# Joining two projection weights, turning softmax weights through DRAM, and a bias product by array quarters in a mixture-of-experts kernel

## The chip, the cores and the metric

The kernel runs on one core of one Trainium2 chip, in f32 throughout. The metric is the device time of one launch in microseconds; the median of three runs of the kernel before is 474.62 us (474.44 to 474.79).

## The reference

Eight batches of 512 tokens of width 256 attend to 64 context rows each; a router then mixes three experts, and a gate multiplies the result. Cut to what matters:

```python
nx = layer_norm(x, ln_gamma, ln_beta)                 # (8, 512, 256)
q, k, v = nx @ Wq, context @ Wk, context @ Wv         # context (8, 64, 256)
weights = softmax(q @ k.T * H ** -0.5)                # (8, 512, 64)
evidence = weights @ v
combined = concat([nx, evidence, anchor])             # anchor: one row for each batch
probs = softmax(combined @ router_W + router_b)       # 3 experts
h = silu(combined @ e_w1 + e_b1)                      # (8, 512, 3, 512)
routed = sum((h @ e_w2 + e_b2) * probs)
g = sigmoid(silu(combined @ gate_w1 + gate_b1) @ gate_w2 + gate_b2)
out = x + g * (routed @ out_w + out_b)
```

## The kernel before

**Work and order.** Batches go in four pairs, j = 0 to 3. Before the loop comes a start: the context and the attention weights are loaded and projected, and the first pair is normalized, scored and softmaxed. Then for every pair come the gate's first layer, three expert layers (e = 0, 1, 2, each with points A to D) and the outputs (points named "begin", "gate", P1, P5, P6, P2, P7, P3, P4 in that order). The order on every engine is written out by hand: instructions stand in each engine's queue in the order in which the program issues them, and an engine works its queue in that order. Small steps for the next pair are hung on the points by `put(within, ...)` and `put(between, ...)` (lines 1119 to 1184). Products over a pair of batches are made by a scheme of seven products with sums and differences (`nx_product`, `product`, line 657), with tokens as 512 columns.

**Attention.** q is never made. `context_transposes` turns the context, `project_keys` (line 303) makes the keys kT from Wk, `wq_transposes` (line 285) turns Wq, and `project(wqT, kT, keep_m, "m")` (line 1088) makes m = Wq k, so that `scores` (line 522) multiply the normalized x by m. The result m lies in mr beside the router's rows for x. The values vT come from `project(wv_sb, ...)` (line 1079); `value_weights` (line 623) multiplies them by the experts' first weights, so that evidence enters the experts as softmax weights times a 64-row product (`evidence`, line 664). For that the softmax weights w must stand with context rows on partitions: `transpose_w` (line 557) does it with four TensorE transposes to PSUM and a ScalarE copy (line 566), for pair 0 in the gate layer and for the later pairs at point P7 of the pair before.

**The start's order.** SyncE's queue loads the context in two halves, then x of batch 0, Wq, x of batch 1, then the first-layer weights (lines 1059 to 1071). ScalarE's queue loads Wk and Wv. VectorE makes statistics of x (`statistics`, line 450), ScalarE the deviation (line 461, which needs a table load for Sqrt), VectorE normalizes (line 469); TensorE transposes x (line 491). `small_transposes` (line 257) turns the bias rows into `cols` and the condition into condT; `router_anchor` (line 324) needs condT.

**Blocks.** VectorE's transpose turns 32x32 blocks. Where a whole turn is wanted, `load_blocks` (line 382) loads from DRAM with the blocks already regrouped, one DMA for 32 partitions, and VectorE turns each block. x of the later batches goes that way: `store_x` (line 494), `regroup_x` (line 498), `transpose_blocks` (line 503). Outputs are turned the same way in `finish` (line 957), and SyncE stores them.

**Biases.** `second_bias` (line 431) multiplies the experts' second biases by out_w once, at point B of expert 0 of pair 0. `anchor_rows` (line 347) multiplies by the condition in array quarters: a 32-column stationary operand, with the result on partitions 32 i to 32 i + 31 of PSUM, and a VectorE transpose that turns it back.

**Pools.** The large tiles of the hidden layer double as scratch in the start (scr_w, scr_k, scr_ctx). The tiles w, wT and vw of the work pool have one buffer each, yb has two. `misc` and `either` (lines 103 and 244) hand out PSUM banks in rotation.

Of the kernel before, what the change touches and what calls it, by code (L numbers as in the profile page):

```python
# [8 lines left out]
F32 = mybir.dt.float32  # L9
# [7 lines left out]
def kernel(  # L17
# [85 lines left out]
    def misc(name):  # L103
        spare.append(spare.pop(0))
        return bank(spare[-1], name)
# [26 lines left out]
    def rows_of(w):  # L132
        return w.rearrange("(k p) n -> p k n", p=P)
# [8 lines left out]
    def by_k(flat, n):  # L142
        return flat.rearrange("p (k n) -> p k n", n=n)
# [3 lines left out]
    scr = scratch(1, 1, "scr_w")  # L147
    wk_sb, wq_sb, wqT, wv_sb = (by_k(scr[:, i * KH * H : (i + 1) * KH * H], H) for i in range(4))
    scr = scratch(0, 2, "scr_k")
    kT = by_k(scr[:, :HK], B * CT)  # L150
    rrow = scr[:E, HK : HK + B]
    scr = scratch(0, 0, "scr_wa0")
    wa = {0: by_k(scr[:, :HK], RH), E: by_k(scr[:, HK : HK + KH * H], H)}
# [90 lines left out]
    def either(name):  # L244
        turn[0] += 1
        return bank((1, 2, 0, 3)[turn[0] % 4], name)
# [10 lines left out]
    def small_transposes():  # L257
        pt = either("pt_rows")
        nc.tensor.transpose(pt[:, :NR], rows, ident[:NR, :NR])
        nc.vector.tensor_copy(cols, pt[:, :NR])  # L260
        pt = either("pt_cond")
        for k in range(KH):
            nc.tensor.transpose(
                pt[:, k * B : (k + 1) * B], cond_sb[:, k * P : (k + 1) * P], ident[:B, :B]
            )
        nc.vector.tensor_copy(
            condT[:, :, :B], pt[:, : KH * B].rearrange("p (k b) -> p k b", b=B)
        )
# [13 lines left out]
            half = slice(d * NX // 2 * P, (d + 1) * NX // 2 * P)  # L282
            (nc.scalar.copy if d else nc.vector.tensor_copy)(ctxT[:, :, half], pt)

    def wq_transposes():
        pt = either("pt_wq")
        for k in range(KH):
            for i in range(KH):
                nc.tensor.transpose(
                    pt[:, k * H + i * P : k * H + (i + 1) * P], wq_sb[:, i, k * P : (k + 1) * P], ident  # L290
                )
        nc.scalar.copy(wqT.rearrange("p k n -> p (k n)"), pt)

    def project(w_sb, src, evacuate, name):
        for m in range(KH):
            ps = either(f"ps_{name}_{m}")
            for k in range(KH):
                nc.tensor.matmul(  # L298
                    ps, w_sb[:, k, m * P : (m + 1) * P], src[:, k, :], start=(k == 0), stop=(k == KH - 1)
                )  # L300
            evacuate(m, ps)

    def project_keys():

        ps = [either(f"ps_k_{m}") for m in range(KH)]
        for d in range(2):
            half = slice(d * NX // 2 * P, (d + 1) * NX // 2 * P)
            for m in range(KH):
                for k in range(KH):
                    nc.tensor.matmul(  # L310
                        ps[m][:, half], wk_sb[:, k, m * P : (m + 1) * P], ctxT[:, k, half],
                        start=(k == 0), stop=(k == KH - 1),
                    )
        for m in range(KH):
            nc.scalar.copy(kT[:, m, :], ps[m])

    def keep_m(m, ps):
        nc.vector.tensor_copy(mr[:, m, :, :CT], ps.rearrange("p (b c) -> p b c", c=CT))
# [54 lines left out]
    w2o = const.tile([P, NE, H], F32, tag="w2o", name="w2o")  # L373
    w2s = const.tile([P, 3, NE // 2, P], F32, tag="w2s", name="w2s")
    b2o = const.tile([P, KH, E], F32, tag="b2o", name="b2o")
    ow_sb = const.tile([P, KH, H], F32, tag="ow_sb", name="ow_sb")
    gw2_sb = const.tile([P, KH, H], F32, tag="gw2_sb", name="gw2_sb")
    gw2s = const.tile([P, 3, P], F32, tag="gw2s", name="gw2s")
# [3 lines left out]
    def load_blocks(dst, src):  # L382

        for k in range(KH):
            for i in range(P // TB):
                lo = k * P + i * TB
                nc.sync.dma_start(
                    dst[i * TB : (i + 1) * TB, k, :].rearrange("r (j c) -> r j c", c=TB),  # L390
                    src[:, lo : lo + TB].rearrange("(j r) c -> r j c", r=TB),
                )
# [37 lines left out]

    def second_bias():

        ps = misc("ps_b2o")
        for i in range(KH):
            for k in range(KH):
                nc.tensor.matmul(
                    ps[:, i * E : (i + 1) * E], ow_sb[:, k, i * P : (i + 1) * P], b2_c[:, :, k],
                    start=(k == 0), stop=(k == KH - 1),
                )
        nc.vector.tensor_copy(b2o, ps[:, : KH * E].rearrange("p (i e) -> p i e", e=E))  # L440
        for i in range(KH):
            nc.vector.tensor_scalar(
                b2o[:, i, 1:], b2o[:, i, 1:], b2o[:, i, 0:1], None, ALU.subtract
            )
        nc.vector.tensor_tensor(b2o[:, :, 0], b2o[:, :, 0], ob_c, ALU.add)
# [105 lines left out]
    def softmax(b):  # L551
        w, sm = S["w", b // 2][:, :, b % 2, :], S.pop(("sm", b))
        rs = work.tile([P, NT], F32, tag="rs", name=f"rs_{b}")
        nc.vector.reciprocal(rs, sm)
        nc.vector.tensor_tensor(w, w, rs.unsqueeze(2).to_broadcast([P, NT, CT]), ALU.mult)

    def transpose_w(j):

# [498 lines left out]
    with tc.manual_schedule(engines=None):  # L1057
        ctx_rows = context.flatten_outer_dims().rearrange("(t p) d -> p t d", p=P)
        for d in range(2):
            half = slice(d * NX // 2, (d + 1) * NX // 2)  # L1060
            nc.sync.dma_start(ctx_sb[:, half, :], ctx_rows[:, half, :])
        nc.scalar.dma_start(wk_sb, rows_of(Wk))
        nc.scalar.dma_start(wv_sb, rows_of(Wv))
        load_x(0)
        nc.sync.dma_start(wq_sb, rows_of(Wq))
        load_x(1)
        for g in (E, 0):
            load_first(g)
# [3 lines left out]

        wake(7)
        context_transposes()
        project_keys()
        statistics(0, 0, NT)
        deviation(0, 0)
        normalize(0)
        project(wv_sb, ctxT, lambda m, ps: nc.scalar.copy(vT[:, m, :], ps), "v")
        small_transposes()  # L1080
        wq_transposes()
        transpose_x(0)
        router_anchor()
        statistics(1, 0, NT)
        deviation(0, 1)
        normalize(1)
        load_table(AF.Exp)
        project(wqT, kT, keep_m, "m")
        combine_weights(E)
        value_weights(0, E)  # L1090
        spread_router_rows(0)
# [22 lines left out]
        for j in range(NP):  # L1114
# [37 lines left out]
            if j + 1 < NP:  # L1152
                b0, b1 = 2 * j + 2, 2 * j + 3
                put(within, "gate", load_x, b0)
                put(within, "gate", load_x, b1)
                put(within, (0, "A" if j else "D"), statistics, b0, 0, NT)
                put(within, (0, "C") if j else (1, "A"), statistics, b1, 0, NT)
                for i in range(2):
                    put(within, (1, "C"), deviation, j + 1, i)
                where = (1, "D") if j else (2, "B")  # L1160
                put(within, where, normalize, b0)
                put(within, where, store_x, b0)
                put(within, where, regroup_x, b0)
                put(within, (2, "C"), normalize, b1)
                put(within, (2, "C"), store_x, b1)
                put(between, "begin", transpose_blocks, b0)
                put(between, "gate", regroup_x, b1)
                put(between, "P1", scores, b0)
                put(between, "begin", value_weights, j + 1, E)
                put(between, "begin", spread_router_rows, j + 1)  # L1170
                put(between, "P5", softmax, b0)
                put(between, "P5", transpose_blocks, b1)
                put(between, "P6", router_logits, b0)
                put(between, "P2", scores, b1)
                put(between, "P2", softmax, b1)
# [47 lines left out]
```

## Time and profile before

| What | Value |
|---|---|
| Median of three runs | 474.62 us |
| The profiled execution | 474.75 us |
| Its span, first to last instruction | 473.0 us |
| Granted TensorE clock over the span | 1.0 |
| DMA engines' mean busy share from 10.4 to 15.7 us | 1.08 |
| The same from 135 to 140 us | 0.30 |
| TensorE busy from 21 to 28 us | 6.71 of 7.00 us |
| VectorE busy from 125 to 155 us | 27.51 of 30.00 us |

The profile is of one execution. Times are microseconds from the span's start. PE is TensorE's matmul, PEld its weight load, DVE is VectorE, ACT is ScalarE, POOL is GpSimd, SPq is SyncE's queue of DMA issues. Busy time counts time in which at least one instruction of the engine runs. A chain piece gives its start and length; the chain is followed back from the last instruction, at each step to what released it, or to the instruction before it on its engine. A timeline line gives start, length, engine, line and operation, output and inputs with their shapes, and in brackets the idle time just before with its releaser. A DMA line gives the issue alone; its landing is in another view. One f32 matmul instruction appears as two records on TensorE, a transpose as one. "x16" means 16 records.

### The profile page before, as it was taken

The page shows a single profiled execution, that of the slowest core. Times are in us where ns is not written, and L with a number is a line of the kernel's source. Part 1 is how long each engine was busy: PE and PEld are TensorE (multiplying, and loading weights), DVE is VectorE, ACT ScalarE, POOL GpSimd, SP SyncE. Part 2 cuts the span into 40 slices and gives each one's busy share as a digit, 9 for nine tenths or more (in the row PEclk, how much of TensorE's full clock was granted, in tenths as well). Part 3 has the DMA queues.
Part 4 walks back from the last instruction along what each step waited for, and adds up shares of the span by engine and source line. Part 5 has one row for each costly group of instructions (what it writes and reads, how often), then busy time and mean ns, then how long its engine had stood idle before and what let it go on. Part 6 is the DMA issues. An engine that isn't in the chain of part 4 may idle for free.

```text
span 473.0 us, 4654 instructions
## 1 busy us (share of the span) xinstructions
PE 467.0 (99%) x1447; PEld 222.8 (47%) x1447; DVE 353.3 (75%) x649; ACT 218.3 (46%) x391; POOL 85.7 (18%) x109
## 2 busy tenths in 40 slices
PE   8999999999999999999999999999999999999997
PEld 6654546445454444445454444445454344444454
DVE  2855846989989555889989565898989624797982
ACT  3555656557221546648320456758221365458000
POOL 5328133200062300000062300000042400000020
PEclk9999999999999999999999999999999999999999
DMA  9988330057211740342111750252111560000013
GB/s 289 366 130 162 54 136 0 0 110 105 27 22 25 164 147 0 82 97 45 17 24 22 158 154 1 66 113 46 18 22 22 84 184 0 1 0 1 0 22 67
DMA packets 118504, 35.27 MB, mean 75 GB/s; under 512 B 105164, under 2 KB 115472, under 8 KB 117968
## 3 DMA queue, kind: packets, MB, share of 16 engines
q1 hardware_dynamic: 114736, 27.02, 27.7%
q0 software_dynamic: 1856, 7.18, 5.1%
q10 hardware_dynamic: 1888, 0.79, 0.6%
q8 instruction: 11, 0.18, 0.2%
q14 instruction: 13, 0.11, 0.1%
HBM read 27.57 MB, written 7.40 MB: 74 GB/s over the span
## 4 chain that ended last, share of the span: by engine, by line
PE 92%; DVE 5%; DMA 1%; ACT 1%; issue 0%; SPq 0%; ACTq 0%; DVEq 0%
PE ps_u L657 42%; PE ps_z L657 18%; PE ps_y L657 15%; PE ps_vw L632 5%; PE ps_gu L657 3%; PE ps_w2o L415 2%; PE ps_s L530 2%; PE ps_gz L657 1%; DVE h L931 1%; DMA scr_ctx<-in_ctx_dram 1%; DVE h L740 1%; PE ps_k L310 1%; PE ps_gy L657 1%; PE ps_v L298 1%; ACT w L545 1%; DVE r L940 0%
## 5 line engine op out<-in xcount | busy, mean ns | idle before, releaser
L740 DVE TENSOR_TENSOR h<-h,pb 128x512 f32<-128x512 f32 x96 | 61.9, 694 | 10.5 <-ACT h L690 10.5
L657 PE MATMUL ps_u<-h,w2o 128*128 128x512 f32 x144 | 63.9, 593 | 0.0
L657 PE MATMUL ps_u<-nxT,w 128*128 128x512 f32 x112 | 55.6, 607 | 0.0
L690 ACT ACTIVATE h<-h,abias 128x512 f32<-128x512 f32 x72 | 49.3, 718 | 8.7 <-DVE h L696 8.2
L657 PE MATMUL ps_z<-wT,vw 64*128 64x512 f32 x104 | 49.5, 605 | 0.0
L963 POOL TENSOR_TENSOR yb<-yb,xb 128x512 f32<-128x512 f32 x14 | 19.1, 1366 | 148.8 <-DVE yb L962 144.5
L657 PE MATMUL ps_z<-h,w2s 128*128 128x512 f32 x96 | 42.8, 595 | 0.2 <-DVE r L946 0.2
L699 ACT COPY h<-ps_u 128x512 f32<-128x512 f32 x48 | 27.9, 582 | 32.0 <-PE ps_u L657 31.6
L657 PEld LDWEIGHTS ps_u<-h,w2o 128*128 128x128 f32 x144 | 27.1, 190 | 31.3 <-issue 29.7
L696 DVE TENSOR_TENSOR h<-h,ps_y 128x512 f32<-128x512 f32 x24 | 16.4, 683 | 28.5 <-PE ps_y L657 24.7
L931 DVE TENSOR_TENSOR h<-h,h 128x1024 f32<-128x1024 f32 x24 | 34.3, 1485 | 0.0
L657 PEld LDWEIGHTS ps_u<-nxT,w 128*128 128x128 f32 x112 | 19.9, 189 | 29.7 <-issue 22.8
L690 ACT ACTIVATE h<-ps_u,abias 128x512 f32<-128x512 f32 x24 | 16.5, 687 | 30.2 <-PE ps_z L657 30.2
L657 PE MATMUL ps_y<-nxT,w 128*128 128x512 f32 x56 | 28.6, 592 | 0.0
L657 PE MATMUL ps_z<-T,ws 128*128 128x512 f32 x56 | 28.6, 592 | 0.0
L657 PEld LDWEIGHTS ps_z<-h,w2s 128*128 128x128 f32 x96 | 17.9, 190 | 22.1 <-issue 21.1
L657 PE MATMUL ps_u<-wT,vw 64*128 64x512 f32 x56 | 27.8, 611 | 0.0
L337 POOL DMA_DIRECT2D vrd<-vw x4 | 3.2, 802 | 133.1 <-ACT vw L639 133.1
L657 PE MATMUL ps_y<-wT,vw 64*128 64x512 f32 x56 | 27.0, 596 | 0.0
L632 PE MATMUL ps_vw<-w,vT 128*128 128x512 f32 (+1 forms) x64 | 26.9, 541 | 0.0
L657 PE MATMUL ps_u<-T,ws 128*128 128x512 f32 x56 | 26.7, 594 | 0.0
L657 PE MATMUL ps_u<-T,w 128*128 128x512 f32 x56 | 26.6, 592 | 0.0
(203 smaller groups left out, 796.4 us busy)
## 6 DMA issues: line engine op xcount, KB each, us to landing
pb<-pd POOLq DMA_DIRECT2D x4, 1536.0 KB, 6.8
x<-in_x_dram SPq DMA_DIRECT2D x8, 512.0 KB, 6.4
xb<-in_x_dram SPq DMA_DIRECT2D x64, 64.0 KB, 2.4
out_dram<-yb SPq DMA_DIRECT2D x56, 64.0 KB, 2.0
w<-in_L_xcond_e_w_dram SPq DMA_DIRECT2D x6, 512.0 KB, 9.3
xd<-x SPq DMA_DIRECT2D x6, 512.0 KB, 3.0
xg<-xd SPq DMA_DIRECT2D x48, 64.0 KB, 2.4
scr_wa<-in_L_xcond_e_w_dram SPq DMA_DIRECT2D x3, 512.0 KB, 5.1
```

The source lines that it names most:

```text
L298: nc.tensor.matmul(ps, w_sb[:, k, m * P : (m + 1) * P], src[:, k, :], start=(k == 0), stop=(k == KH - 1))
L310: nc.tensor.matmul(ps[m][:, half], wk_sb[:, k, m * P : (m + 1) * P], ctxT[:, k, half], start=(k == 0), stop=(k == KH - 1),)
L415: nc.tensor.matmul(ps[:, d * H : (d + 1) * H], w2T[:, k, (i + d) * P : (i + d + 1) * P], ow_sb[:, k, :], start=(k == 0), stop=(k == KH - 1),)
L530: nc.tensor.matmul(ps[:, t, :], nxT[:, k, t * P : (t + 1) * P], mr[:, k, b, :], start=(k == 0), stop=(k == KH - 1),)
L632: nc.tensor.matmul(ps, vT[:, k, j * 2 * CT : (j + 1) * 2 * CT], w1[:, KH + k, n0:n1], start=(k == 0), stop=(k == KH - 1),)
L657: nc.tensor.matmul(ps, lhsT, rhs, start=start, stop=True, skip_group_check=not start)
L690: nc.scalar.activation(h, h if src is None else src, AF.Silu, bias=abias[:, c, 2 * j + i : 2 * j + i + 1])
L696: nc.vector.tensor_tensor(h, h, part, ALU.add)
L699: nc.scalar.copy(chunk(n, i, d), part)
L740: nc.vector.tensor_tensor(h, h, S["pb", j][:, i, 2 * q // RC, :], ALU.mult)
L931: nc.vector.tensor_tensor(d, p, m, ALU.subtract)
L963: nc.gpsimd.tensor_tensor(yb, yb, S["xb", 2 * j + row][:, i, :], ALU.add)
```

## The change

The change has three parts.

**Wk and Wq joined, Wv ahead of x.** The keys are no longer made. Wk and Wq are both turned by `transpose_weights`, `join_keys` multiplies them into wkqT (256 x 256), and m is wkqT applied to the context. Wq is loaded on ScalarE's queue after Wk; Wv moves to SyncE's queue ahead of x of batch 0. The projection of v is split around the join. The Sqrt table is loaded at the front; the statistics of batch 1 are split in two and moved ahead of the transposes of batch 0, and the deviation of batch 1 ahead of `router_anchor`.

**Softmax weights turned through DRAM.** For pairs 1 to 3, `transpose_w` at P7 goes. `regroup_w` at P2 stores w to DRAM and loads it back with its 32x32 blocks regrouped, both on SyncE's queue; `transpose_w_blocks` at P3 turns the blocks on VectorE. Pair 0 keeps `transpose_w`.

**Second bias by array quarters.** GpSimd zeroes and fills b2T, 32 columns wide, TensorE multiplies by quarters of the array, and VectorE turns the result.

```diff
-    kT = by_k(scr[:, :HK], B * CT)
+    wkT, wkqT = (by_k(scr[:, i * KH * H : (i + 1) * KH * H], H) for i in range(2))
...
         nc.vector.tensor_copy(cols, pt[:, :NR])
+        nc.gpsimd.tensor_copy(b2T[:, :, :E], b2_c.rearrange("p e k -> p k e"))
...
-    def wq_transposes():
-        pt = either("pt_wq")
+    def transpose_weights(dst, w_sb, name):
+        pt = either(f"pt_{name}")
...
-        nc.scalar.copy(wqT.rearrange("p k n -> p (k n)"), pt)
+        nc.scalar.copy(dst.rearrange("p k n -> p (k n)"), pt)
...
-    def project_keys():
-
-        ps = [either(f"ps_k_{m}") for m in range(KH)]
-        for d in range(2):
-            half = slice(d * NX // 2 * P, (d + 1) * NX // 2 * P)
-            for m in range(KH):
-                for k in range(KH):
-                    nc.tensor.matmul(
-                        ps[m][:, half], wk_sb[:, k, m * P : (m + 1) * P], ctxT[:, k, half],
-                        start=(k == 0), stop=(k == KH - 1),
-                    )
+    def keep_v(m, ps):
+        nc.scalar.copy(vT[:, m, :], ps)
+
+    def join_keys():
+
+        ps = either("ps_kq").rearrange("p (m n) -> p m n", n=H)
         for m in range(KH):
-            nc.scalar.copy(kT[:, m, :], ps[m])
+            for k in range(KH):
+                nc.tensor.matmul(
+                    ps[:, m, :], wkT[:, k, m * P : (m + 1) * P], wqT[:, k, :],
+                    start=(k == 0), stop=(k == KH - 1),
+                )
+        nc.scalar.copy(wkqT, ps)
...
+    b2T = const.tile([P, KH, QB], F32, tag="b2T", name="b2T")
+    nc.gpsimd.memset(b2T, 0.0)
...
     def second_bias():
 
-        ps = misc("ps_b2o")
-        for i in range(KH):
-            for k in range(KH):
+
+        ps = misc("ps_b2o")[:, : KH * QB]
+        for k in range(KH):
+            w = ow_sb[:, k, :].rearrange("p (c i f) -> p i c f", i=P // QB, f=QB)
+            for i in range(P // QB):
                 nc.tensor.matmul(
-                    ps[:, i * E : (i + 1) * E], ow_sb[:, k, i * P : (i + 1) * P], b2_c[:, :, k],
-                    start=(k == 0), stop=(k == KH - 1),
+                    ps[i * QB : (i + 1) * QB, :].rearrange("p (c f) -> p c f", f=QB),
+                    b2T[:, k, :], w[:, i, :, :], start=(k == 0), stop=(k == KH - 1),
                 )
-        nc.vector.tensor_copy(b2o, ps[:, : KH * E].rearrange("p (i e) -> p i e", e=E))
+        blocks = setup.tile([P, KH * QB], F32, tag="ar", name="b2b")
+        nc.vector.transpose(blocks, ps)
+        nc.vector.tensor_copy(b2o, blocks.rearrange("p (i e) -> p i e", e=QB)[:, :, :E])
...
+    def regroup_w(j):
+
+        wd = dram.tile([T, P], F32, tag="wd", name=f"wd_{j}")
+        nc.sync.dma_start(
+            wd.rearrange("(t p) c -> p t c", p=P), S["w", j].rearrange("p t i c -> p t (i c)")
+        )
+        S["wg", j] = work.tile([P, 1, T], F32, tag="wg", name=f"wg_{j}", bufs=1)
+        load_blocks(S["wg", j], wd)
+
+    def transpose_w_blocks(j):
+        S["wT", j] = work.tile([P, T], F32, tag="wT", name=f"wT_{j}", bufs=1)
+        nc.vector.transpose(S["wT", j], S.pop(("wg", j))[:, 0, :])
...
-        nc.scalar.dma_start(wk_sb, rows_of(Wk))
-        nc.scalar.dma_start(wv_sb, rows_of(Wv))
+        for w_sb, w in ((wk_sb, Wk), (wq_sb, Wq)):
+            nc.scalar.dma_start(w_sb, rows_of(w))
+        nc.sync.dma_start(wv_sb, rows_of(Wv))
+        load_table(AF.Sqrt)
         load_x(0)
-        nc.sync.dma_start(wq_sb, rows_of(Wq))
         load_x(1)
...
         context_transposes()
-        project_keys()
+        transpose_weights(wkT, wk_sb, "wk")
+        transpose_weights(wqT, wq_sb, "wq")
         statistics(0, 0, NT)
         deviation(0, 0)
         normalize(0)
-        project(wv_sb, ctxT, lambda m, ps: nc.scalar.copy(vT[:, m, :], ps), "v")
+        project(wv_sb, ctxT, keep_v, "v", (0,))
+        join_keys()
+        project(wv_sb, ctxT, keep_v, "v", (1,))
+        statistics(1, 0, NT // 2)
         small_transposes()
-        wq_transposes()
+        statistics(1, NT // 2, NT)
         transpose_x(0)
+        deviation(0, 1)
         router_anchor()
-        statistics(1, 0, NT)
-        deviation(0, 1)
         normalize(1)
         load_table(AF.Exp)
-        project(wqT, kT, keep_m, "m")
+        project(wkqT, ctxT, keep_m, "m")
...
+                put(between, "P2", regroup_w, j + 1)
                 put(between, "P2", combine_x, j + 1, nc.gpsimd)
-                put(between, "P7", transpose_w, j + 1)
                 put(between, "P7", value_weights, j + 1, 0)
                 put(between, "P7", router_logits, b1)
                 put(between, "P3", value_weights, j + 1, 1)
+                put(between, "P3", transpose_w_blocks, j + 1)
```

`load_blocks` now loops over as many 128-column groups as its target has, one for w.

More of the change, by code (lines that the diff above doesn't have):

```diff
@@ L289, in wq_transposes, with project @@
                 nc.tensor.transpose(
-                    pt[:, k * H + i * P : k * H + (i + 1) * P], wq_sb[:, i, k * P : (k + 1) * P], ident
+                    pt[:, k * H + i * P : k * H + (i + 1) * P], w_sb[:, i, k * P : (k + 1) * P], ident
                 )
-        nc.scalar.copy(wqT.rearrange("p k n -> p (k n)"), pt)
-    def project(w_sb, src, evacuate, name):
-        for m in range(KH):
+        nc.scalar.copy(dst.rearrange("p k n -> p (k n)"), pt)
+    def project(w_sb, src, evacuate, name, ms=range(KH)):
+        for m in ms:
             ps = either(f"ps_{name}_{m}")
@@ L301, in project @@
             evacuate(m, ps)
-    def project_keys():
-        ps = [either(f"ps_k_{m}") for m in range(KH)]
-        for d in range(2):
-            half = slice(d * NX // 2 * P, (d + 1) * NX // 2 * P)
-            for m in range(KH):
-                for k in range(KH):
-                    nc.tensor.matmul(
-                        ps[m][:, half], wk_sb[:, k, m * P : (m + 1) * P], ctxT[:, k, half],
-                        start=(k == 0), stop=(k == KH - 1),
-                    )
-        for m in range(KH):
-            nc.scalar.copy(kT[:, m, :], ps[m])
+    def keep_v(m, ps):
+        nc.scalar.copy(vT[:, m, :], ps)
+    def join_keys():
+        ps = either("ps_kq").rearrange("p (m n) -> p m n", n=H)
+        for m in range(KH):
+            for k in range(KH):
[4 more added lines that the diff above has]
+        nc.scalar.copy(wkqT, ps)
     def keep_m(m, ps):
@@ L382, in load_blocks @@
     def load_blocks(dst, src):
-        for k in range(KH):
+        for k in range(dst.shape[1]):
             for i in range(P // TB):
@@ L431, in second_bias @@
     def second_bias():
-        ps = misc("ps_b2o")
-        for i in range(KH):
-            for k in range(KH):
+        ps = misc("ps_b2o")[:, : KH * QB]
+        for k in range(KH):
+            w = ow_sb[:, k, :].rearrange("p (c i f) -> p i c f", i=P // QB, f=QB)
+            for i in range(P // QB):
                 nc.tensor.matmul(
-                    ps[:, i * E : (i + 1) * E], ow_sb[:, k, i * P : (i + 1) * P], b2_c[:, :, k],
-                    start=(k == 0), stop=(k == KH - 1),
-                )
-        nc.vector.tensor_copy(b2o, ps[:, : KH * E].rearrange("p (i e) -> p i e", e=E))
+                    ps[i * QB : (i + 1) * QB, :].rearrange("p (c f) -> p c f", f=QB),
+                    b2T[:, k, :], w[:, i, :, :], start=(k == 0), stop=(k == KH - 1),
+                )
+        blocks = setup.tile([P, KH * QB], F32, tag="ar", name="b2b")
+        nc.vector.transpose(blocks, ps)
+        nc.vector.tensor_copy(b2o, blocks.rearrange("p (i e) -> p i e", e=QB)[:, :, :E])
         for i in range(KH):
```

## The prediction

> **What bounds the kernel now.** I read the page first (busy time, the chain that ended last), then the chain piece by piece over the first 60 us, then each engine's timeline at the two places that the change touches, the start and the passage from one pair of batches to the next.
>
> ```profile
> span 473.0 us, 4654 instructions
> PE 467.0 (99%) x1447; PEld 222.8 (47%) x1447; DVE 353.3 (75%) x649; ACT 218.3 (46%) x391; POOL 85.7 (18%) x109
> PE 92%; DVE 5%; DMA 1%; ACT 1%; issue 0%; SPq 0%; ACTq 0%; DVEq 0%
> ```
>
> TensorE (PE) is busy in 99% of the span and makes 92% of the chain. So TensorE work that goes is time that goes, unless TensorE only reaches a wait earlier. The chain's pieces (start, length) price that work and show where others hold TensorE:
>
> ```profile
> 1.23 5.01 DMA scr_ctx<-in_ctx_dram
> 6.94 3.46 PE ps_k L310 x16
> 10.40 3.43 PE ps_v L298 x8
> 14.11 0.59 PE pt_wq L289 x4
> 18.82 1.38 DVE x L469 x4
> 20.20 1.20 DVE mr L318 x2
> 24.79 2.48 ACT w L545 x16
> 27.31 0.64 PE ps_ar L355 x16
> 27.95 1.06 PE ps_u L657 x2
> 29.87 0.44 PE pt_w L563 x4
> 47.79 0.79 PE ps_b2o L436 x8
> 50.40 0.57 PE ps_ar L355 x16
> ```
>
> Each f32 matmul shows as two records, so keys are 8 matmuls of 256 columns at 0.43 us, and a 512-column one costs 0.86. Four 128x128 transposes cost 0.44. From 15 to 27 us the chain runs through VectorE (DVE) and ScalarE (ACT): a cut in TensorE's start work pays only if these come earlier too.
>
> ```profile
> 8.01 0.43 DVE L457 BATCH_NORM_STATS2 st<-x 128x6 f32<-128x256 f32 x1 [1.68 <-DMA x<-in_x_dram]
> 12.66 0.18 DVE L466 RECIPROCAL rstd<-sd 128x4 f32<-128x4 f32 x1 [2.42 <-ACT sd L461]
> 135.41 0.18 DVE L554 RECIPROCAL rs<-sm 128x4 f32<-128x4 f32 x1 [1.42 <-ACT w L545]
> 151.00 0.42 DVE L646 TENSOR_TENSOR vw<-vw 64x256 f32<-64x256 f32 x1
> 156.65 0.69 DVE L696 TENSOR_TENSOR hg<-hg,ps_u 128x512 f32<-128x512 f32 x1 [0.87 <-PE ps_u L657]
> ```
>
> VectorE's first statistics wait for x until 8.01; its 2.42 us of idling before 12.66 is ScalarE's table load. At the passage VectorE works without a gap from 135.41 to 155.78 and then idles 0.87: that is the room for a new VectorE instruction.
>
> ```profile
> 95.79 0.39 SPq L496 DMA_DIRECT2D xd<-x  x1
> 99.10 4.03 SPq L389 DMA_DIRECT2D xg<-xd  x8
> ```
>
> This is SyncE's queue doing to x what the change does to the softmax weights: 3.3 us from the store's issue to the first load's, then 0.5 us a load.
>
> **What the Trainium skill says.** "VectorE: DVE Perf Modes", "The three transpose paths": VectorE transposes only inside 32x32 blocks, hence the detour through DRAM; the trace has this operation at 0.71 us for 128x512 (L962), 0.69 from regrouped blocks (L508). "DMA: Bandwidth & Descriptors", "Two DMAs through the same engine are not ordered": the issuer must await the store before it reads back; the 3.3 us gap agrees. "ScalarE: Activation LUTs", "What ACT_TABLE_LOAD costs": about 1283 ns a load; the trace has 1.28. "TensorE: Matmul & The Clock Gate", "Part 4: PE-mode transpose": transposes don't count as TensorE being busy for its clock; in the trace the 8 context transposes with idle gaps (4.98 to 6.94) leave the clock at 1.0.
>
> **The start.** Removed: the keys (3.46 us, 8 matmuls of 256), their two ScalarE copies. Added: 4 transposes of Wk (0.44), the join of 4 matmuls of 256 (1.73), two ScalarE copies in place of two. Wq's transposes and Wv's halves only move. TensorE saves 3.46 - 2.17 = 1.29. The queues: Wq takes Wv's place on ScalarE's queue (landing 5.3 us after issue at 1.28, so near 7.1). Wv goes on SyncE's queue past x of batch 0; behind it are both x loads and all first weights. x0's 512 KB landed at 7.95; Wv with 256 KB ahead lands near 7.5, x0 near 8.9, where Wq landed before (issue 2.24 plus 6.7), and x1 and later loads stay, as the bytes ahead of them are the same. The Sqrt table load goes ahead of the first copy, where a load stood at 1.79 anyway; the one at 11.04 disappears.
>
> New order from 6.94, with the durations above: Wk transposes to 7.38, Wq to 7.82, first half of v 9.54, join 11.27, second half 12.99, small transposes (0.28) 13.27. VectorE: x0 at 8.9, four statistics pairs 2.24 to 11.2, deviation at once 11.5, reciprocal and normalize (1.6) to 13.2, just ahead of TensorE, which transposes x0 (0.9) to 14.17. Statistics of x1 now go two and two around the small copies; so condT comes at 14.6 and TensorE waits 0.4 for it, router anchor to 14.75. VectorE ends x1's statistics at 15.7, scales x0 to 16.5, normalizes x1 from 16.7 to 18.3 (20.2 before), mr to 19.6 (21.4 before). TensorE: product m (3.43) to 18.2, value weights (0.88) 19.05, x1 transposes 19.95, both scores (twice 1.73) 23.4 with mr in time (before, it waited), value weights 25.15, anchor rows to 26.2, waiting for ScalarE's last exponential near 25.5 (27.3 before). The main part begins at 26.2 instead of 27.95: 1.75. Since x0 has 0.05 us of slack in this, I take 1.6; from below 0.4 (TensorE's saving mostly waited away), from above 2.1. ScalarE's queue: Wk's and Wq's turned copies end at 8.8, ahead of the join at 9.54; the deviation waits there to 11.2 with v's and the join's copies behind it, which end at 12.7, ahead of their use at 14.75. SyncE's loads that wait for the weights' scratch (issued at 19.46) may start near 13, which buys nothing while the DMA share is 1.0 (to 28 us). GpSimd: one memset and one copy of b2T (its 128x6 copy L238 took 0.29) stand ahead of the router's DMA; that waits for a VectorE result at 16.5 as before (16.39), so nothing. If that cover failed, 0.3 on a DMA whose reader comes at 44.5.
>
> **Second bias.** 8 records at 128 weight columns, 0.79 us, become 16 by array quarters with 64 columns. The nearest row, anchor rows of 128 columns by quarters, takes 0.57 for 16; the 64-column ones have 0.4 busy. I take 0.35: gain 0.44. VectorE gets a transpose more (128x64, 0.22). Behind it are router logits and the w2 transposes, and TensorE already meets those at 54.6 in the chain, with VectorE ending them (L407, 53.60 and 1.30 long) at 54.9; so 0.2 of the gain is waited for: 0.24 net, bounds 0 and 0.6.
>
> **The passages**, three of them. TensorE loses 4 transposes (0.44), ScalarE a copy (0.59, hidden). Gain 3 x 0.44 = 1.33. SyncE gets a store and 4 loads between two groups of output stores: softmax ends at 136.7, first load 140.0, last issue 142, landing (2.5) 144.5. Queued behind are the next output stores, which wait for GpSimd at 146 anyway. VectorE reaches the transpose at 151.4: 7 us to spare. There it costs 0.69 (lone) to 1.5 (an L575 product stretched from 0.56 beside GpSimd), ahead of the last finish, the router and the gate's sums. The 0.87 idle takes 0.7; the product at 156.5 that needs the turned weights comes 5 us after. I take 0 lost; without that cover 0.4 each. Bounds of the gain 0.1 to 1.5.
>
> **Sum**: 1.6 + 0.24 + 1.33 = 3.2. The profiled execution took 474.75 (span 473.0, 1.75 around it), so 471.55; the median of the runs, 474.62, is 0.13 lower: 471.4.
>
> **The rivals.**
> Half pays (472.6): x0, delayed by Wv, or VectorE holds the start and the 1.6 shrinks to 0.4. For it: x0's tiny slack and the chain's VectorE pieces there. Against: 2.42 us of VectorE idling go with the table load.
> The clock gives way (473.1): TensorE has little but transposes from 4.4 to 7.8, and runs at half speed for one 3.4 us window (the Trainium skill's TensorE page, "Part 1: The HAM clock gate", has this length), losing 1.7; two windows bring 474.8, no change. Against: clock 1.0 through the shorter stretch now; no row shows 3.4 us of it.
> The turned weights are late (479): the DRAM round trip stalls VectorE at its transpose, and TensorE behind it. It decides from a landing at 155.4, 18.7 us after the softmax; each later us costs 1 us in each passage, and 1.1 us eats all gain. At 158, 3 x 2.6 = 7.8, less 3.2: 4.6 slower. For it: the small hop through DRAM at 24.5 took 9.8 us to land. Against: that was under full DMA load; at 137 the DMA share is 0.30.
>
> **The numbers.** Forecast 0.63 (own range 470.6 to 472.2), half pays 0.23, clock 0.07, late 0.07. The range 470.3 to 473.0 has all gains at their upper bound below and the half case above. A measurement tells 0.2% (0.95 us) from no change: faster 0.63 + 0.23 + 0.02 = 0.88, same 0.05, slower 0.07.
>
> **What would show it.** Right: ps_u L657's first piece near 26.2; statistics starting near 8.9; no pt_w at the three passages and a VectorE transpose near 151 that waits for no DMA; the passage's product at 156.5 less about 2.3. Wrong: TensorE idle for x or condT beyond 0.5 us, a clock below 1.0 near 8 us, TensorE waiting for wT.

## The result, and the profile after

The changed kernel takes 472.03 us (median of 6 runs, 471.86 to 472.56) against 474.69 for the kernel before (474.44 to 474.98, 6 runs). The ratio is 0.9947, 95% interval [0.9934, 0.9959]. The forecast was 471.4; 2.7 us were gained of the 3.2 that the sum had. The profiled execution of after took 472.56, the slowest of its six, with a span of 470.4 at a granted clock of 1.0.

From the page of after: the span, the busy time, and the shares of the chain that ended last.

```profile
span 470.4 us, 4664 instructions
PE 465.1 (99%) x1439; PEld 221.1 (47%) x1439; DVE 353.8 (75%) x653; ACT 215.4 (46%) x388; POOL 85.1 (18%) x111
PE 91%; DVE 4%; SPq 3%; DMA 0%; issue 0%; ACT 0%; ACTq 0%
```

TensorE has 1.9 us less to do and still is busy in 99% of a shorter span. The 3% of SPq in the chain lie between 33.9 and 49.5 us: followed back from a wait of TensorE's at 52.91, the chain runs into SyncE's loads of x, although VectorE, which ends that wait, shows no idle time from 42.7 us on. The chain over the first 28 us of after (start, length, what) shows how the start changed.

```profile
4.45 1.09 PE pt_ctx L278 x4
...
6.93 0.57 PE pt_wk L290 x4
7.50 0.44 PE pt_wq L290 x4
7.94 1.72 PE ps_v L299 x4
9.66 1.73 PE ps_kq L312 x8
11.38 1.72 PE ps_v L299 x4
...
13.38 1.02 PE pt_x L498 x8
...
14.58 3.63 PE ps_m L299 x8
...
19.96 3.54 PE ps_s L537 x32
...
24.41 1.30 ACT w L552 x8
...
25.76 0.64 PE ps_ar L356 x16
26.40 1.06 PE ps_u L677 x2
```

From 6.93 to 23.5 every piece is TensorE's: up to the softmax the chain no longer passes through VectorE, which before held it from 15 us on. The main part (first ps_u) begins at 26.40 instead of 27.95.

The passage from pair 0 to pair 1, from the timelines of SyncE's queue, VectorE and TensorE in after (start, length, engine, line and operation, output and inputs, and in brackets the idle time before):

```profile
135.38 0.38 SPq L567 DMA_DIRECT2D wd<-w  x1
137.69 1.91 SPq L392 DMA_DIRECT2D wg<-wd  x4
...
149.99 0.71 DVE L575 STREAM_TRANSPOSE wT<-wg 128x512 f32<-128x512 f32 x1
...
154.77 0.69 DVE L716 TENSOR_TENSOR hg<-hg,ps_u 128x512 f32<-128x512 f32 x1
...
156.06 0.59 PE L677 MATMUL ps_y<-wT,vw 64*128 64x512 f32 x1
...
156.49 0.59 PE L677 MATMUL ps_u<-wT,vw 64*128 64x512 f32 x1
```

The transpose has no idle time before it: the weights had landed long before. The sum at 154.77 had 0.87 of idle time ahead of it before and has none now, and TensorE goes on without a gap. What went there from TensorE stands in the chain at the head of the passage, in before and then in after:

```profile
137.14 0.44 PE pt_w L563 x4
...
144.45 1.72 PE ps_vw L632 x4
```

```profile
135.71 1.72 PE ps_vw L652 x4
...
142.57 1.72 PE ps_vw L652 x4
```

**Where the time went**, in the two profiles. Start: 1.55. Passages: 7.31, 7.34 and 7.34 us before from the transposes of w to the second ps_vw, and 6.86, 6.87 and 6.87 after from the first ps_vw to the second, so 1.39 in all. From the start of the main part to the end of the w2 products (the experts' second weights times out_w): 30.29 before and 30.40 after, so 0.1 was lost there, where the second bias stands. That makes 2.83, and the last store's issue comes 2.84 earlier (470.05 and 467.21). But the span ends 3.2 us after that issue instead of 2.9, and 2.1 us instead of 1.75 lie outside the span. These two, 0.3 and 0.35, are gains given back where no row of the trace has an instruction.

### The profile page after: what moved, and what is told of

Its sections match the earlier page's. It is cut to its first block, busy times and chain, and to the rows that moved or that the text cites. A ratio compares the mean times of both kernels' runs of the same rounds, so it can differ in the third digit from the quotient of the medians.

```text
span 470.4 us, 4664 instructions
## 1 busy us (share of the span) xinstructions
PE 465.1 (99%) x1439; PEld 221.1 (47%) x1439; DVE 353.8 (75%) x653; ACT 215.4 (46%) x388; POOL 85.1 (18%) x111
## 4 chain that ended last, share of the span: by engine, by line
PE 91%; DVE 4%; SPq 3%; DMA 0%; issue 0%; ACT 0%; ACTq 0%
PE ps_u L677 40%; PE ps_z L677 17%; PE ps_y L677 14%; PE ps_vw L652 4%; SPq L392 3%; PE ps_gu L677 3%; PE ps_s L537 3%; PE ps_w2o L418 2%; PE ps_gz L677 1%; DVE h L951 1%; PE ps_wake L255 1%; DVE h L760 1%; PE ps_m L299 1%; PE ps_v L299 1%; PE ps_gy L677 1%; DVE r L960 0%
## 5 line engine op out<-in xcount | busy, mean ns | idle before, releaser
L677 PE MATMUL ps_z<-wT,vw 64*128 64x512 f32 x104 | 49.5, 605 | 0.0
L677 PE MATMUL ps_z<-nxT,ws 128*128 128x512 f32 x56 | 26.6, 592 | 0.0
```

The lines of the kernel that those rows point to most:

```text
L677: nc.tensor.matmul(ps, lhsT, rhs, start=start, stop=True, skip_group_check=not start)
```

## The experiments

All times are medians; each ratio is to the runs of the kernel before on the same chip. "Outside" is the time of a run less its span.

**The three parts alone.** The kernel before with the new start only, with the passages only, with the second bias only; and the changed kernel with the old second bias. The first three take over the lines of the change's diff for their part and no others. The last one's edit:

```diff
-    b2T = const.tile([P, KH, QB], F32, tag="b2T", name="b2T")
-    nc.gpsimd.memset(b2T, 0.0)
...
-        nc.gpsimd.tensor_copy(b2T[:, :, :E], b2_c.rearrange("p e k -> p k e"))
...
     def second_bias():
...
-                    ps[i * QB : (i + 1) * QB, :].rearrange("p (c f) -> p c f", f=QB),
-                    b2T[:, k, :], w[:, i, :, :], start=(k == 0), stop=(k == KH - 1),
+                    ps[:, i * E : (i + 1) * E], ow_sb[:, k, i * P : (i + 1) * P], b2_c[:, :, k],
+                    start=(k == 0), stop=(k == KH - 1),
...
-        blocks = setup.tile([P, KH * QB], F32, tag="ar", name="b2b")
-        nc.vector.transpose(blocks, ps)
-        nc.vector.tensor_copy(b2o, blocks.rearrange("p (i e) -> p i e", e=QB)[:, :, :E])
+        nc.vector.tensor_copy(b2o, ps[:, : KH * E].rearrange("p (i e) -> p i e", e=E))
```

Start alone. 

> The start's part alone on the kernel before (old second bias, TensorE transposes at all passages). My theory, from the two traces, where TensorE's main part begins at 26.40 instead of 27.95: 1.5 to 2.0 us faster than the kernel before, about 473.0, main part near 26.4 and the w2 products (ps_w2o) 1.5 us earlier than before with no wait on VectorE longer than before. Rival: the parts need each other and the start alone gives under 0.8, about 474.

Passages alone. 

> The softmax weights turned through DRAM alone on the kernel before. My theory: three times 0.44 to 0.48 us of TensorE go, nothing comes back: 1.4 us faster, about 473.3, the start untouched. Rival: the extra DMAs lengthen what lies outside the span or the last stores (after has 2.1 us outside its span against 1.75 before): then only 1.0 faster, 473.7.

Second bias alone. 

> The second bias by array quarters alone on the kernel before. My theory: TensorE's piece shrinks from 0.79 to about 0.37, of which 0.2 is waited for at the w2 products, because VectorE has one instruction more: 0.2 faster, about 474.5, at the edge of what can be told. Rival: the whole 0.4 arrives, 474.3; other rival: nothing arrives, 474.7.

All but the second bias. 

> The changed kernel with the old second bias. My theory now: in the changed kernel VectorE holds TensorE at the first w2 product, so TensorE's shorter piece only makes it wait there, and the old bias costs nothing: 472.0 as the changed kernel, within 0.2, with the wait of ps_w2o on VectorE gone. Rival: TensorE's 0.4 us count as the prediction had it, partly: 0.24 to 0.44 slower than the changed kernel, 472.3 to 472.5.

| Kernel | us | Ratio, interval | Outside, us | Last issue to end, us |
|---|---|---|---|---|
| start alone | 472.80 | 0.9964 [0.9950, 0.9977] | 1.8 | 2.9 |
| passages alone | 473.35 | 0.9976 [0.9967, 0.9985] | 1.8 | 3.2 |
| second bias alone | 474.52 | 1.0005 [0.9997, 1.0013] | 2.07 to 2.17 | 2.9 |
| all but the second bias | 471.68 | 0.9940 [0.9928, 0.9953] | 1.8 | 3.2 |
| after | 472.03 | 0.9947 [0.9934, 0.9959] | 2.06 to 2.16 | 3.2 |

By the ratios the parts add: 1.7 and 1.1 gained and 0.2 lost make 2.6, against 2.5 for after. The passages alone gain 1.1 of the expected 1.4: TensorE's rows give back 1.4, and the last stores, as the rival had it, take 0.3 (the 473.35 fits the theory's 473.3 only because the kernel before took 474.46 beside these runs, less than the expectation counted from). The second bias alone lands at the expected 474.5, but a ratio just above 1 says that it gains nothing: its spans are 0.3 shorter (medians 472.4 and 472.7), and its runs lie outside the span by 0.3 more, which was not expected. Without it the change takes 471.68: 0.3 under its expectation, and the fastest version of this study. Its interval and that of after overlap, so the runs alone don't settle the 0.35. The column "outside" shows where most of it is, as it is 1.8 in every kernel of this table with the old second bias and above 2.05 in both with the new.

**What brings the time outside the span.** The kernel before with GpSimd's two instructions of the new second bias, whose result nothing reads; the old products stay.

```diff
+        nc.gpsimd.tensor_copy(b2T[:, :, :E], b2_c.rearrange("p e k -> p k e"))
...
+    b2T = const.tile([P, KH, QB], F32, tag="b2T", name="b2T")
+    nc.gpsimd.memset(b2T, 0.0)
```

> The kernel before with only GpSimd's share of the new second bias: one memset and one copy of b2T, which nothing reads; the old products stay. The kernels with the new second bias take 2.06 to 2.17 us outside the span, those without it 1.72 to 1.85. If GpSimd's two instructions bring that (theory), this one takes about 2.1 outside the span and 474.9 to 475.0 in all. If the quarter products or VectorE's turn bring it (rival), 1.8 outside and 474.6, as before.

474.93 us (13 runs), ratio 1.0006 [0.9998, 1.0014]. GpSimd's timeline has the two instructions with 0.37 us between them, off the chain:

```profile
8.74 0.18 POOL L378 MEMSET b2T<- 128x64 f32 x1
...
14.40 0.19 POOL L261 COPY b2T<-cols 128x6 f32<-128x6 f32 x1 [0.49 <-DVE condT L267]
```

The span is 472.9, as in before, and each run lies 2.06 to 2.16 outside it, against 1.72 to 1.83 for the kernel before beside it. So the 0.3 us come with these two instructions, not with the products or the turn. Which of the two it is, and what the chip does in that time, stays open.

**What the second bias meets.** The main part comes earlier and GpSimd's sums of weights do not, so in after VectorE's two router products stand beside more of them and take 0.83 and 0.64 instead of 0.52 and 0.56; I held this for the reason why VectorE ends the w2 transposes late. The experiment takes the read of the router rows of pair 0 behind GpSimd's first sums, so that these run earlier.

```diff
+        if j == 0:
+            S["vrd"] = vrd
+        else:
+            read_router_rows(j, vrd)
+
+    def read_router_rows(j, vrd):
...
         combine_weights(2)
+        read_router_rows(0, S.pop("vrd"))
```

> The changed kernel with GpSimd's weight sums (12 instructions) ahead of its wait for the router rows' round trip through DRAM, into its idle 10 us. Theory: in the changed kernel these sums run beside VectorE's router product (0.83 and 0.64 us instead of 0.52 and 0.56) and so hold the w2 products; moved, the product takes 0.52 and 0.56 again and the time falls by 0.3 to 0.5, to 471.6. Rival: beside the softmax at 24 to 33 us the sums slow VectorE just as much, the main part starts later, and the time stays at 472.0 or rises.

472.03 us (6 runs), ratio 0.9945 [0.9931, 0.9960]: no difference, as the rival had it. That doesn't clear the overlap. The router products are back at 0.52 and 0.56, and the wait at the w2 products gets shorter: from the start of the ps_z products ahead of them to the first of them it is 1.72 us in before (52.72 to 54.44), where nothing waits, 2.07 in after (50.84 to 52.91) and 1.86 here (51.17 to 53.03). But the sums now run beside the softmax of the start, and TensorE waits there for ScalarE's last exponential. In after, and then in this kernel:

```profile
25.76 0.64 PE L356 MATMUL ps_ar<-scr_wa,condT 128*32 128x128 f32 x16 [0.15 <-ACT w L552]
```

```profile
25.80 0.64 PE L362 MATMUL ps_ar<-scr_wa,condT 128*32 128x128 f32 x16 [0.64 <-ACT w L558]
```

From Wk's transposes to the main part it takes 19.89 us (19.47 in after), and from there to the second bias 0.3 more than in after. So 0.2 gained at the w2 products meets 0.7 lost ahead of them in this profile, and the run can't say what the overlap costs by itself. Start alone shows it from the other side: with the old second bias, but router products of 0.73 and 0.98, the w2 products wait as well (2.02 us from 50.56 to 52.58), which its expectation had ruled out; in all but the second bias the products take 0.52 and 0.71, and nothing waits (1.72 us). The Trainium skill names the overlap: "GPSIMD Engine Reference", "1. Specifications", says that GpSimd shares its SBUF interfaces with VectorE's instructions that have two SBUF inputs, which the router products have.

The other part is VectorE's list. Its timeline in this kernel, and then in after with TensorE's row:

```profile
47.00 0.25 DVE L452 STREAM_TRANSPOSE b2b<-ps_b2o 128x64 f32<-128x64 f32 x1 [0.18 <-PE ps_b2o L447]
...
52.27 1.30 DVE L416 STREAM_TRANSPOSE scr_w2T<-scr_w 128x512 f32<-128x512 f32 x2
```

```profile
46.89 0.24 DVE L446 STREAM_TRANSPOSE b2b<-ps_b2o 128x64 f32<-128x64 f32 x1
...
52.16 1.30 DVE L410 STREAM_TRANSPOSE scr_w2T<-scr_w 128x512 f32<-128x512 f32 x2
...
52.91 3.88 PE L418 MATMUL ps_w2o<-ow_sb,scr_w2T 128*128 128x256 f32 x16 [0.20 <-DVE scr_w2T L410]
```

In this kernel VectorE is early enough to wait for the bias (0.18), and it needs from 47.00 to 53.57 for its work up to the end of the w2 transposes, 6.6 us. In before the same stretch without the extra turn was 48.61 to 54.90, 6.3. TensorE needs 6.0 for its own part (48.57 to 54.60 in before), and its w2 products start when the first of the two transposes is through (in after 52.16 and half of 1.30). So TensorE, which is through with the bias 0.43 sooner, waits for VectorE even where nothing slows that. The chain, in second bias alone and then in before:

```profile
47.53 0.36 PE ps_b2o L441 x16
...
54.01 3.87 PE ps_w2o L418 x16
```

```profile
54.60 3.64 PE ps_w2o L415 x16
```

From the bias to the end of the w2 products it takes 10.35 us there and 10.45 in before (from 47.79): of 0.43 saved, 0.1 is left. The products that wait take 3.86 to 3.88 instead of 3.64, in every kernel with a wait; that is 0.23 of what is lost, and why it is so stays open. In after the overlap takes some 0.2 more, by the 2.07 and 1.86 above (one profile of each), and the 0.1 gained becomes the 0.1 lost.

**The start: table, order of loads, place of the statistics.** Three edits, the first to the changed kernel, the others to the version with the old second bias. The table load at the front taken away, so that it stands at the first deviation:

```diff
-        load_table(AF.Sqrt)
```

> The changed kernel without the Sqrt table load at the front; the load then stands before the deviation. The prediction credited the table load with VectorE's 2.42 us of idling in the kernel before. Theory now: in the changed kernel ScalarE's queue is empty from 8.6 us to the deviation at 10.67, so the 1.28 us fit there and nothing changes (472.0, within 0.2); the idling went because the copies of the keys no longer stand ahead of the deviation. Rival, the prediction's words: the load delays the deviation by its 1.28 us, normalize ends at 13.8 instead of 12.6 and TensorE waits 0.5 us for x0.

472.20 us (4 runs), ratio 0.9950 [0.9934, 0.9966]: no difference. ScalarE's timeline shows why:

```profile
8.02 1.28 ACT L468 ACT_TABLE_LOAD   x1
10.72 0.30 ACT L468 ACTIVATE sd<-mv,eps_t 128x4 f32<-128x4 f32 x1 [1.42 <-DVE mv L465]
```

The load fits into the time in which ScalarE waits for the statistics, with 1.42 to spare. In before the copies of the keys were ahead of it in the queue:

```profile
10.43 0.58 ACT L315 COPY scr_k<-ps_k 128x512 f32<-128x512 f32 x1 [0.28 <-PE ps_k L310]
11.04 1.28 ACT L461 ACT_TABLE_LOAD   x1
12.33 0.30 ACT L461 ACTIVATE sd<-mv,eps_t 128x4 f32<-128x4 f32 x1
```

VectorE's statistics were through at 10.24 there, the second copy at 11.01. With the copies in place, the load moved ahead would have given 1.3 of the 2.42 us (an estimate from these rows; no run has it).

x of batch 0 ahead of Wv:

```diff
-        nc.sync.dma_start(wv_sb, rows_of(Wv))
         load_table(AF.Sqrt)
         load_x(0)
+        nc.sync.dma_start(wv_sb, rows_of(Wv))
```

> The changed kernel with the old second bias, x of batch 0 loaded ahead of Wv on SyncE's queue, the rest the same. Theory: Wv then lands near 8.9, where x0 and 256 KB more stood in the prediction, and TensorE, which reaches v at 7.4 to 7.9, waits about 1.0 us for it; x0 near 7.95 helps nobody: 472.7. Rival: x0 was the load that held the start, and its earlier landing gives up to 0.4: 471.3. A third: the two orders are worth the same, 471.7.

472.87 us (5 runs), ratio 0.9963 [0.9950, 0.9975]: 1.2 slower than 471.68, as the theory had it (and 1.1 slower than the version with one more store below, which ran beside it). From the timeline of this kernel, and its list of DMA issues (size, us to landing):

```profile
7.56 0.43 DVE L457 BATCH_NORM_STATS2 st<-x 128x6 f32<-128x256 f32 x1 [1.54 <-DMA x<-in_x_dram]
...
8.58 1.96 PE L298 MATMUL ps_v<-scr_ctx,scr_w 128*128 128x512 f32 x4 [1.19 <-DVE st L457]
```

```profile
scr_w<-in_L_xcond_Wv_dram SPq DMA_DIRECT2D x1, 256.0 KB, 6.2
```

TensorE idles 1.19 us ahead of v. The row names a VectorE step that v doesn't use. It is Wv's load: issued at 2.25, behind x, it lands 6.2 us later, at 8.45, just ahead of v; in all but the second bias it landed at 6.7. The statistics start 0.5 earlier than in that version (8.07) and nobody gains.

The statistics and the deviation of batch 1 in their old places:

```diff
-        statistics(1, 0, NT // 2)
         small_transposes()
-        statistics(1, NT // 2, NT)
         transpose_x(0)
-        deviation(0, 1)
         router_anchor()
+        statistics(1, 0, NT)
+        deviation(0, 1)
```

> The changed kernel with the old second bias and the old places of the statistics and the deviation of batch 1 (behind the transposes of batch 0 and the router's anchor). Theory: the small copies and the condition then come earlier (13.3 for VectorE's two copies anyway), but x1's normalization ends 0.3 later or so, and TensorE has the value weights and x1's transposes between; so within 0.3 of 471.7, at most 472.0. Rival: the statistics' place is where most of the start's 1.6 comes from, because mr waits behind them as before: 472.7 or more.

472.23 us (5 runs), ratio 0.9946 [0.9933, 0.9958]: 0.5 slower, between the two and over the 472.0 that the theory allowed. The chain of this kernel runs through VectorE again:

```profile
16.87 0.31 ACT sd L461
...
17.42 1.38 DVE x L469 x4
18.80 1.20 DVE mr L318 x2
```

From Wk's transposes to the main part it takes 19.81 us; with the new places 19.37. That is 0.44: more than I thought, and less than most of the gain.

**The passage's cover.** The round trip through DRAM begun later, at P7 of the passage instead of P2; and the turn done three times instead of once.

```diff
-                put(between, "P2", regroup_w, j + 1)
...
+                put(between, "P7", regroup_w, j + 1)
```

> The changed kernel with the DRAM round trip of the softmax weights issued at P7, behind the second group of output stores, instead of P2. It lands near 153 us in the first passage where VectorE reaches its transpose at 150.0. Theory: VectorE stands 3 us there, everything behind it shifts, and TensorE, which may wait 1 us at most, loses about 2 us in each of three passages: 477.7. Rival: VectorE makes it up before TensorE needs it, under 1 us in all.

```diff
-        nc.vector.transpose(S["wT", j], S.pop(("wg", j))[:, 0, :])
+        for _ in range(3):
+            nc.vector.transpose(S["wT", j], S["wg", j][:, 0, :])
+        S.pop(("wg", j))
```

> The changed kernel with VectorE's block transpose made three times over in each passage (same result, 1.3 us more of VectorE). In the trace VectorE has no idle left before the gate's sum, but the sum ends 1.0 us ahead of TensorE's need of the bank. Theory: 0.3 us lost in each passage, 0.9 in all: 472.9. Rivals: VectorE is on the path already, 1.3 lost in each, 3.9 in all: 475.9; or it has more room than I read, nothing lost.

Late: 477.81 us (4 runs), ratio 1.0067 [1.0050, 1.0083], slower than before as expected. Three turns: 473.56 us (16 runs), ratio 0.9979 [0.9972, 0.9986], 1.5 over after. VectorE's and TensorE's timelines, of the late kernel first:

```profile
152.57 0.71 DVE L575 STREAM_TRANSPOSE wT<-wg 128x512 f32<-128x512 f32 x1 [2.90 <-DMA wg<-wd]
...
157.16 0.68 DVE L716 TENSOR_TENSOR hg<-hg,ps_u 128x512 f32<-128x512 f32 x1
...
155.76 0.59 PE L677 MATMUL ps_y<-wT,vw 64*128 64x512 f32 x1
...
157.90 0.69 PE L677 MATMUL ps_u<-wT,vw 64*128 64x512 f32 x1 [1.54 <-DVE hg L716]
```

```profile
149.54 2.21 DVE L576 STREAM_TRANSPOSE wT<-wg 128x512 f32<-128x512 f32 x3
...
155.63 0.68 DVE L718 TENSOR_TENSOR hg<-hg,ps_u 128x512 f32<-128x512 f32 x1
...
155.60 0.59 PE L679 MATMUL ps_y<-wT,vw 64*128 64x512 f32 x1
...
156.37 0.69 PE L679 MATMUL ps_u<-wT,vw 64*128 64x512 f32 x1 [0.17 <-DVE hg L718]
```

Both price the cover, that is, how much later VectorE may be before TensorE waits. In the late kernel the sum starts 2.39 later than in after while TensorE is 0.30 earlier; TensorE, due at 155.76 and 0.43 (one record), starts 1.71 late: 2.69 less 1.71 is 0.98 of cover. With three turns it is 0.86 and 0.46 later, 1.32; TensorE starts 0.34 late: 0.98 again. In the second and third passage the same product starts 1.92 and 1.65 late in the late kernel, 0.41 and 0.42 with three turns, and each time it takes 0.1 longer (0.69 for 0.59). That makes 5.6 and 1.5 us, and the medians lie 5.8 and 1.5 over after; the two profiles' spans differ from after's by less (475.7 and 471.4 against 470.4), as after's profiled execution came to its main part 0.4 to 0.7 later than theirs. The late kernel cost what the theory had; three turns cost 0.5 a passage instead of 0.3. So in the changed kernel VectorE has 1.0 us left at a passage, and what it loses beyond that TensorE loses too, and 0.1 more, though the product that reads the turned weights first is not what waits: it is the sum behind the turn, which frees a bank of PSUM.

**The last stores.** In all kernels with the passages the last stores land later. The version with the old second bias, and one more store of 128 rows of 256 bytes in the first passage:

```diff
+        if j == 1:
+            wx = dram.tile([P, CT], F32, tag="wx", name="wx")
+            nc.sync.dma_start(wx, S["w", j][:, 0, 0, :])
```

> The changed kernel with the old second bias, and one small store (128 rows of 256 bytes) to DRAM more at the first passage. Theory: the slower last landing of the kernels with the passages (3.16 to 3.22 us from the last issue to the end, against 2.91 to 2.95 without them) comes from where the last stores fall among SyncE's transfers in turn, the passages adding 15, so that a sixteenth restores it: 2.93 to the end, 471.4 in all. Rival: it comes from something else, and stays 3.2, 471.7.

471.75 us (5 runs), ratio 0.9942 [0.9928, 0.9955], and 3.3 us from the last issue to the end: nothing is restored, and the theory of the turns falls. From the list of DMA issues from 460 us on (size, median us to landing), SyncE's last stores in before and then in after:

```profile
out_dram<-y SPq DMA_DIRECT2D x2, 64.0 KB, 1.7
out_dram<-hg SPq DMA_DIRECT2D x2, 64.0 KB, 2.4
```

```profile
out_dram<-y SPq DMA_DIRECT2D x2, 64.0 KB, 1.9
out_dram<-hg SPq DMA_DIRECT2D x2, 64.0 KB, 2.7
```

The same stores, with little else under way than as many on ScalarE's queue, land 0.2 to 0.3 later. The passages bring it (passages alone has 1.9 and 2.7 as well, start alone 1.7 and 2.4); why stays open.

## Why the prediction was right, and where it was off

**The start: 1.6 forecast, 1.55 found** between the two profiles, and 1.64 with the old second bias (19.37 us from Wk's transposes to the main part, against 21.01 from the keys in before). The times of the new order held: product m at 14.58 (forecast 14.75), both scores at 19.96 (19.95), the main part at 26.40 (26.2) behind ScalarE's last exponential at 25.72 (25.5). Steps inside were wrong without harm to the sum. "2.42 us of VectorE idling go with the table load": ScalarE's timeline in before has the load behind the keys' copies, and in the changed kernel, without these, moving the load is worth nothing. Wq's landing "near 7.1" doesn't follow from 1.28 and 5.3, which make 6.6; it landed at 6.16. And x of batch 0 was there for VectorE at 8.41, not 8.9, so that condT was ready at 13.8 and TensorE did not wait 0.4 for it; what this gave went into transposes and a product m that took 1.02 and 3.63 instead of 0.9 and 3.43. The order of the loads was treated as a risk to x; Wv's place ahead of x is what the new order of products needs most, as 1.2 of the 1.6 go without it. The rival "half pays" had the right engine, VectorE, and the statistics' place is what keeps it off the chain, for 0.44.

**The second bias: 0.24 gain forecast, about 0.4 lost.** This is the term that was mis-sized. TensorE's part was right (0.79 to 0.36, forecast 0.35). The step "so 0.2 of the gain is waited for" took VectorE to be through with its share in time for the rest of the gain, and did not add up VectorE's list from the bias on. Second bias alone shows 0.3 gone of 0.43, since VectorE has 6.6 us of work from the bias to the end of the w2 transposes and TensorE 6.0. With the main part earlier, GpSimd's sums slow VectorE's router products, and some 0.2 more goes; the prediction summed the parts without this meeting. And "GpSimd: so nothing" was wrong by 0.3 us, which no row of the trace could show, because they lie outside the span.

**The passages: 1.33 forecast, 1.39 found**, in TensorE's rows as worked out. The cover was larger than the 0.87 named: the turn takes 0.71, and 1.0 is still free. The last stores' 0.3 us come off, which the sum had not. The rival "the turned weights are late" had the right wait and too late a point: its 155.4 is refuted by the late kernel, where a landing near 152.5 costs 1.8 us in the first passage. By the cover of 1.0 it decides from a turn that starts near 151, 15.6 us after the store's issue; the loads are issued by 139.6, and land 2.3 later, so 9 us are to spare.

**The clock** stayed at 1.0 in the records, and the rival's loss of 1.7 us did not come. Yet a slower pace where the rival looked for it shows in the rows: after's eight context transposes took 1.09 and 1.12 us instead of 0.63 and 0.66, and Wk's 0.57 instead of 0.44. Two kernels with the old start have it too (see the last section), so the change did not bring it. It is not in the start's 1.55, because in before the context landed 0.5 later (6.24 and 5.77), and both profiles come to their weights at 6.9.

**In all**, 1.55, 1.39 and -0.1 are 2.8, against 3.2; 0.3 and 0.35 behind the last issue leave 2.2 between the two profiled executions. The total fell within the range because the two large terms came out at their sizes; the second bias had the wrong sign, and what was lost behind the last issue stood in no term. The medians give 2.66, because the profiled execution of after was half a microsecond slower than its median.

## What to carry to other kernels

Ask of every saved microsecond of the bound engine who is next at its next wait, and add up that engine's whole list from the common start; a saving that meets a list one instruction longer is mostly given back (0.3 of 0.43 us here). A moved load is judged by the operation of the bound engine that needs it first, not by the busiest reader of the load that it passes. And compare the whole time of a run with its span, since a part of a change can cost where the trace has no rows.

## What the runs showed that was not expected

- Two GpSimd instructions of 0.18 and 0.19 us, off the chain, add 0.3 us outside the span, in all runs of the seven kernels that have them.
- Three round trips through DRAM in the middle of the kernel make the last stores, 64 KB each, land 0.2 to 0.3 us later, though the last of them is issued at 353 us and the stores at 463 and after.
- A granted clock of 1.0 in the records went with two paces at the start: the first four context transposes took 0.63 us in four of fourteen profiles, 0.80 in one and 1.08 or 1.09 in nine, and the second four 0.66 in nine and 0.85 to 1.12 in five. All nine slow ones began by 4.51 us, but so did one of the fast (4.46). Kernels with the old start are among both, so it doesn't hang on the change. The second four stand right ahead of the weights, so by the difference they move a single execution by 0.2 to 0.5 us (an estimate).
